# Graph layer with residual normalisation: 64 edges of each later part with a low source node fetched from a table in SBUF by one-hot products

## The chip, the cores and the metric

The kernel runs on one core of one Trainium2 chip. The metric is device time in microseconds of that core, the median of several runs. One profiled execution is shown beside it; all durations below come from that one.

## The reference, cut to what matters

12,500 nodes with 128 features, 412,500 edges sorted by destination (200,000 random pairs in both directions, and a self-loop for each node, which is the last edge of its destination).

```python
theta = x[dst] - x[src]
w = sigmoid(relu(theta @ W1 + b1) @ W2 + b2)          # W2 has one column
agg = segment_sum(w * theta, dst, num_segments=n_nodes)
indeg = segment_sum(ones, dst, num_segments=n_nodes)
x = layernorm(x + agg + indeg * (x @ W4 + b4))
```

All is float32. A self-loop has theta = 0, so it adds 1 to `indeg` and nothing else.

## The kernel before

A table `z` of 12,500 rows is made first, in 13 chunks (`table_chunk`): each row holds `x @ W1` and `x`, 256 numbers, 1 KB, and is written to DRAM. Since theta @ W1 is a difference of two such rows, an edge needs one gathered row of `z` for its source; what it needs of its destination comes from a window of 96 nodes.

Edges are taken in 394 *parts*. A part fills up to 8 tiles of 128 edges. The first 32 parts (`PLAIN`) hold 1024 edges each. A later part covers `CE` = 1050 edges of which at most 1024 remain, because self-loops are squeezed out. Two parts make a *block* (197 blocks), and a block has one window of 96 destination nodes.

The steps of a part, by the name of the helper and its lines:

- `gather(s)` (L281): one indirect DMA for each tile, issued from GpSimd (POOL), brings 128 rows of `z` into a buffer of `zbuf`. There are `NZ` = 10 such buffers, each as large as one part. Parts 0 to 7 gather `x` instead, two parts to a buffer, since the table is not ready; `both` computes their products.
- `window(b)` (L507 to L536): transposes the 96 nodes' features, multiplies by W1 and W4, and spreads the destination rows with small one-hots `pick` into `y3`. Its products use the PSUM tile `pw`, of which there is one.
- `one_hot(s, half)` (L554, L556): for each half part, TensorE broadcasts the destination offsets into the PSUM tile `pd` (also one), and VectorE compares them into the one-hot `oh`.
- `spread_y(s)` (L565): `oh` times `y3` puts each edge's destination row into the PSUM tile `ph` (two of them).
- `one_hot_w(s)` (L573): a one-hot `ow` from edges to the 96 nodes.
- `weights(s)` (L607 to L614): VectorE subtracts the gathered row (L607), multiplies relu of it by W2 (L608) and sums (L611); ScalarE takes the sigmoid (L612) and scales the 8 tiles by it into `wx` (L614).
- `add_up(s)` (L633): TensorE adds `ow` times `wx` into the block's PSUM tile `pa`; `total(b)` normalises and stores the block.

Gathers run `AHEAD` = 4 parts ahead in the text of the loop; on the chip POOL goes on as long as a buffer of `zbuf` is free, which is when L607 and L614 of the part that had it are done.

The later parts need their self-loops squeezed out before they can be gathered. `place(i, ...)` does that for a *set* of up to 128 parts at once, one part to a partition: it marks edges, and then shifts the kept ones to the left by 1, 2, 4, ... places in 6 passes over chunks of 210 columns (L422, L424, L426: three VectorE instructions for a chunk). It is a generator; the loop over parts takes four steps of it a part for the first set and one step a part for the others, so that its work lies between that of the parts. At its end ScalarE and TensorE turn the result into `src_i` (the gathers' indices), `rel` and `off`. There are three sets; the first is needed by the gathers of part 32.

The order on each engine is made by a scheduler from this program; SP's queue alone keeps the order of the text. At the end a flag, made of checks on the indices (`bad`), decides whether a general path (`any_dst`) computes everything once more.

Of the kernel before, what the change touches and what calls it, by code (L numbers as in the profile page):

```python
# [20 lines left out]
K = 8  # L21
# [7 lines left out]
TG = 7  # L29
NZ = 10  # L30
AHEAD = 4
# [3 lines left out]
PLAIN = 2 * FIRST  # L35
CE = 1050
BIG = 1 << 16
# [5 lines left out]
def gnn_resnorm(  # L43
# [11 lines left out]
    out: bass.AP,  # L55
):


# [64 lines left out]
    def load(i):  # L123

        s0, n, full = sets[i]
        es = ep.tile([P, CE], I32, name="es")
        ed = ep.tile([P, CE + 1], I32, name="ed")
        e0 = E1 + (s0 - PLAIN) * CE
        if full < n:
            nc.vector.memset(es[:n, :], 0)  # L130
            nc.vector.memset(ed[:n, :], N)
        for t, edges, m in ((es, src, CE), (ed, dst, CE + 1)):
            nc.sync.dma_start(t[:full, :m], bass.AP(
                tensor=edges.tensor, offset=edges.offset + e0, ap=[[CE, full], [1, m]]))
            if full < n:
                nc.sync.dma_start(
                    t[full:n, :TAIL], edges[E - TAIL:E].rearrange("(s e) -> s e", s=1))
        bb = ep.tile([P, 1], I32, name="bb")
        with nc.allow_non_contiguous_dma(reason="each block's first dst"):
            nc.sync.dma_start(bb[:n], bass.AP(  # L140
                tensor=dst.tensor, offset=dst.offset + e0, ap=[[SUB * CE, n // SUB], [0, SUB], [1, 1]]))
        return es, ed, bb
# [56 lines left out]
    def constants():  # L199
# [57 lines left out]
        nc.vector.tensor_scalar(at, at, -4.0, None, op0=OP.add)  # L257
        return place_c, one_c, m12, m2, yu_buf, behind, ones_b, b4_3


    wx_buf = [const.tile([P, K, AW], F32, name=f"wx{i}") for i in range(3)]
    for t in wx_buf:
        nc.vector.memset(t[:, :, D + 1:], 1.0)

    zbuf = [const.tile([P, K, 2 * D], F32, name=f"zbuf{i}") for i in range(NZ)]
    NX = NH // 2

    def tiles(s):
        return K if s < NF else KT
# [24 lines left out]

    bad = const.tile([P, 12 + 10 * len(sets)], F32, name="bad")
    nc.vector.memset(bad, 0.0)
# [68 lines left out]
    def place(i, ps, es, ed, bb):  # L365

        s0, n, full = sets[i]
        es, ed, bb = es[:n], ed[:n], bb[:n]  # L370
        v = nc.vector
        c = ep.tile([P, 6], F32, name="col")[:n]
# [6 lines left out]
        v.tensor_sub(c[:, 3:4], nxt, d0)  # L379
        b = bad[:n, 12 + 10 * i:22 + 10 * i]  # L380
        v.tensor_scalar(b[:, 0:1], c[:, 3:4], -float(SW - 1), None, op0=OP.add)
        v.tensor_scalar(b[:full, 1:2], c[:full, 3:4], -1.0, float(CE - BE), op0=OP.mult, op1=OP.add)
        v.tensor_scalar(b[:, 2:3], c[:, 2:3], -1.0, -float(NOT), op0=OP.mult, op1=OP.add)
# [7 lines left out]
        for j in range(3):  # L391
            at = slice(j * C, (j + 1) * C)
            step = ps.tile([P, G, P], F32, name="pw").rearrange("p g d -> p (g d)")[:n, :C]
            v.tensor_sub(step, ed[:, j * C + 1:(j + 1) * C + 1], ed[:, at])
            q = ep.tile([P, C], F32, name="eq")[:n]
            v.tensor_sub(q, es[:, at], ed[:, at])
            yield
            v.tensor_mul(q, q, step)
            v.scalar_tensor_tensor(t[:, at], step, 0.0, t[:, at], op0=OP.is_equal, op1=OP.mult)
            nc.scalar.activation(step, step, AF.Square, accum_out=b[:, 4 + j:5 + j])  # L400
            nc.scalar.activation(q, q, AF.Square, accum_out=b[:, 7 + j:8 + j])
            yield
# [4 lines left out]
        v.memset(b[:, 5:7], 0.0)  # L407
        w = ep.tile([P, CE], I32, name="ew0")[:n]
        v.tensor_add(w, t, es)
        yield  # L410
        def half(w, h):
            return w.bitcast(U16).rearrange("p (e h) -> p e h", h=2)[:, :, h]

        C = CE // 5
        for r in range(SW.bit_length()):
            u = ep.tile([P, CE], I32, name=f"ew{1 - r % 2}")[:n]
            m = 1 << r
            for c0 in range(0, CE, C):
                c2 = min(c0 + C + m, CE)
                c1 = c2 - m  # L420
                bit = bits[:n, :c2 - c0]
                v.tensor_scalar(bit, w[:, c0:c2], BIG.bit_length() - 1 + r, 1,  # L422
                                op0=OP.logical_shift_right, op1=OP.bitwise_and)
                v.scalar_tensor_tensor(u[:, c0:c2], bit, 0.0, w[:, c0:c2],  # L424
                                       op0=OP.is_equal, op1=OP.mult)
                v.copy_predicated(u[:, c0:c1], bit[:, m:m + c1 - c0], w[:, c0 + m:c1 + m])  # L426
                yield
            w = u
        off = pp.tile([P, BE], BF16, name="off")
        nc.scalar.activation(off[:n], half(w, 1)[:, :BE], AF.Identity, bias=c[:, 1:2])  # L430
        t = ep.tile([P, CE], F32, name="et")[:n]
        nc.scalar.activation(t[:, :BE], half(w, 1)[:, :BE], AF.Identity, bias=c[:, 2:3])
        yield
        src_i = pp.tile([P, K, P], I32, name="src_i")
        rel = pp.tile([P, K, P], F32, name="rel")
        f = ep.tile([P, CE], F32, name="es")[:n]
        nc.scalar.activation(f[:, :BE], half(w, 0)[:, :BE], AF.Copy)
        yield
# [10 lines left out]
    with tc.manual_schedule(engines={SP}), tc.tile_pool(name="work", bufs=2) as wp, tc.tile_pool(  # L449
# [57 lines left out]
        def window(b):  # L507
# [14 lines left out]
            for h in range(ns):  # L522
# [12 lines left out]
                                           op0=OP.mult, op1=OP.add)  # L535
            d.update(y3=y3, u=yu[:, 1, :])  # L536

# [30 lines left out]
        def one_hot_w(s):  # L568

            n = tiles(s)  # L570
            (_, rel, _), i = set_of(s)
            ow = wp.tile([P, K, WB], F32, name="ow", bufs=4)
            nc.vector.tensor_tensor(  # L573
# [20 lines left out]
        def weights(s):  # L594
# [4 lines left out]
            wx = wx_buf[s % 3]  # L599
            h = wp.tile([P, K, D], F32, name="h")  # L600
            if s < NH:
# [14 lines left out]
            return summed, scaled  # L616

        def add_up(s):
            n = tiles(s)
# [3 lines left out]
            if h == 0:  # L623
                bd["pa"] = ps_l.tile([P, AW], F32, name="pa")
                if carry[0] is not None:
# [4 lines left out]
                                     start=True, stop=False)  # L630
            end = h == SUB - 1 or s == NS - 1
            for k in range(n):
                nc.tensor.matmul(bd["pa"][:WB], d["ow"][:, k, :], wx_buf[s % 3][:, k, :],  # L633
# [45 lines left out]
        def fetch(b):  # L679
            if b < NK:  # L680
                load_block(b)

        xts, done = [], []

# [13 lines left out]
        with after(done[1]):  # L698
            place_first_dst(0, ps_l, dst_f)
            place_c, one_c, m12, m2, yu_buf, behind, ones_b, b4_3 = constants()  # L700
        fetch(0)
# [10 lines left out]
        for i, (s0, _, _) in enumerate(sets):  # L712
            turns[PLAIN // 4 if i == 0 else s0 - P + AHEAD] = i
        steps = iter(())
# [8 lines left out]
        for s in range(NS + 2):  # L723
            if s in turns:
                edges[s + 3] = turns[s], load(turns[s])
            if s in edges:
                i, loaded = edges.pop(s)
                steps = place(i, ps_l, *loaded)
            for _ in range(4 if s < PLAIN else 1):
                next(steps, None)  # L730
            if s + AHEAD < NS:
# [13 lines left out]
            if s < NS:  # L745
                weighted = weights(s)
            if s + 2 < NS and tiles(s + 2) > G:
                one_hot(s + 2, 1)
            if s > 1:
                with after(weighted if s == NS else [rooted[0]] if s > NS else []):  # L750
                    add_up(s - 2)


# [198 lines left out]
```

## Time and profile before

| | us |
|---|---|
| Median of 3 runs (lowest, highest) | 3978.15 (3977.43, 3979.46) |
| The profiled execution | 3977.41 |
| Its span | 3975.6 |
| Busy: PE, DVE | 2208.2, 2853.7 |
| Busy: ACT, POOL | 1634.7, 2988.3 |
| First and last gather start | 4.1, 3949.6 |

PE is TensorE, PEld its weight load, DVE VectorE, ACT ScalarE, POOL GpSimd, SP SyncE. A line of the page's groups has the source line, the engine, the operation, what it writes and reads, the shapes and the count; after the first bar the busy time in all and the mean in ns of one; after the second the idle time of that engine just before these instructions, and what ended most of it. The line PEclk gives the granted TensorE clock in tenths for 40 equal slices of the span. The granted clock over the whole execution was 0.689 of full.

### The profile page before, as it was taken

To read this page: it belongs to the slowest core of one execution; us is meant where nothing else is said; L and a number is where in the kernel's file an instruction comes from. 1 tells how busy PE (TensorE), PEld (TensorE's weight loads), DVE (VectorE), ACT (ScalarE), POOL (GpSimd) and SP (SyncE) were. 2 spreads that over 40 slices of the span, in tenths; PEclk is the share of its full clock that TensorE was granted. 3 is DMA by queue.
4 is the path that set the end of the run, shared out by engine and by line. 5 is a ranking of instruction groups with operands and counts; after the bars stand their busy time and mean duration, and the time that the engine had idled before them with its cause. 6 is when DMAs were issued, how large, how long until landed. Compare 5 with 4: busy or idle time off the path is not lost.

```text
span 3975.6 us, 46634 instructions
## 1 busy us (share of the span) xinstructions
PE 2208.2 (56%) x12940; PEld 1759.9 (44%) x12941; DVE 2853.7 (72%) x4838; ACT 1634.7 (41%) x5158; POOL 2988.3 (75%) x3159
## 2 busy tenths in 40 slices
PE   6757665655555555556555555555555555555554
PEld 5645444444444444444444444444444444444443
DVE  4798887766666666777776666667666666666675
ACT  3535544443344343444443434433443333344343
POOL 7777777777777777777777777777777777777775
PEclk7867776666666666666666666666666666666666
DMA  7434333333333333433333333333333333333333
GB/s 259 118 110 118 114 111 110 111 111 109 111 110 110 111 110 111 119 107 110 111 109 112 110 111 110 111 109 111 111 110 111 110 110 111 111 110 110 111 111 87
DMA packets 201597, 454.17 MB, mean 114 GB/s; under 512 B 58355, under 2 KB 97755, under 8 KB 199791
## 3 DMA queue, kind: packets, MB, share of 16 engines
q0 software_dynamic: 150176, 408.88, 35.8%
q1 hardware_dynamic: 49181, 35.83, 2.9%
q10 hardware_dynamic: 1970, 6.40, 0.5%
q8 instruction: 104, 1.70, 0.2%
q14 instruction: 166, 1.36, 0.1%
HBM read 428.40 MB, written 22.48 MB: 113 GB/s over the span
## 4 chain that ended last, share of the span: by engine, by line
DVE 42%; DMA 25%; ACT 22%; PE 6%; issue 4%; DVEq 0%; POOL 0%; SPq 0%; ACTq 0%; POOLq 0%
DMA zbuf<-z,src_i 24%; ACT wx L614 18%; DVE ph L607 11%; DVE lg L611 10%; DVE h L608 10%; DVE oh L556 5%; ACT wx L612 3%; PE pa L633 2%; DVE pw L530 2%; DVE y L534 2%; DVE ow L573 1%; DVE o L675 1%; DMA z<-zbuf 1%; PE ph L592 1%; DVEq L607 0%
## 5 line engine op out<-in xcount | busy, mean ns | idle before, releaser
L281 POOL DMA_INDIRECT zbuf<-z,src_i x2894 | 2743.7, 948 | 881.6 <-issue 481.0
L607 DVE TENSOR_TENSOR ph<-ph,zbuf 128x1024 f32<-128x1024 f32 (+1 forms) x386 | 474.8, 1230 | 983.3 <-DMA zbuf<-z,src_i 983.0
L633 PE MATMUL pa<-wx,ow 128*96 128x130 f32 x6300 | 1036.7, 332 | 16.8 <-DVE ow L573 12.8
L633 PEld LDWEIGHTS pa<-wx,ow 128*96 128x96 f32 x6300 | 1009.4, 212 | 48.7 <-DVE ow L573 14.1
L614 ACT ACTIVATE wx<-zbuf,wx 128x128 f32<-128x128 f32 x3150 | 964.0, 388 | 12.2
L565 PEld LDWEIGHTS <-oh 128*128 128x128 bf16 x3086 | 264.2, 112 | 1464.7 <-issue 1393.0
L565 PE MATMUL ph<-y,oh 128*128 128x128 bf16 x3086 | 338.7, 252 | 883.0 <-DVE y L534 777.2
L556 DVE TENSOR_SCALAR oh<-pd,place_c,one_c 128x512 bf16<-128x512 f32 (+1 forms) x788 | 612.9, 778 | 34.6 <-PE ph L590 25.4
L554 PE MATMUL pd<-off,ident_b 128*128 128x512 bf16 (+1 forms) x723 | 351.1, 486 | 510.0 <-DVE oh L556 505.0
L611 DVE TENSOR_REDUCE lg<-h 128x8 f32<-128x1024 f32 x394 | 475.9, 1208 | 2.0 <-ACT wx L612 1.9
L608 DVE SCALAR_TENSOR_TENSOR h<-ph,w_r 128x1024 f32<-128x1024 f32 (+1 forms) x386 | 468.8, 1214 | 0.0
L573 DVE TENSOR_TENSOR ow<-fix,rel 128x768 f32<-128x768 f32 x394 | 371.0, 942 | 0.0
L642 ACT ACTIVATE a<-pa 96x130 f32<-96x130 f32 x197 | 54.3, 276 | 733.1 <-PE pa L633 733.1
L612 ACT ACTIVATE wx<-lg,b_c 128x8 f32<-128x8 f32 x394 | 120.9, 307 | 494.4 <-DVE lg L611 464.5
L532 ACT ACTIVATE ym<-pw 128x256 bf16<-128x256 f32 x197 | 75.4, 383 | 485.4 <-DVE pw L530 483.7
L527 PE MATMUL pw<-yu,pick 99*128 99x128 f32 x788 | 201.6, 379 | 113.0 <-ACT wx L612 49.2
L515 PE MATMUL pw<-wts,xwT 128*96 128x256 f32 x394 | 202.3, 611 | 55.6 <-ACT xwT L513 55.1
L281 POOL DMA_INDIRECT zbuf<-z,src x192 | 182.8, 952 | 58.5 <-issue 33.2
L527 PEld LDWEIGHTS pw<-yu,pick 99*128 99x128 f32 x788 | 145.7, 241 | 157.7 <-issue 58.0
L513 ACT ACTIVATE xwT<-pw 128x96 f32<-128x96 f32 x197 | 49.0, 249 | 278.7 <-PE pw L511 278.4
L629 PEld LDWEIGHTS pa<-a,sh 96*96 96x96 f32 x392 | 96.7, 268 | 125.2 <-DVE sh L627 67.6
L629 PE MATMUL pa<-a,sh 96*96 96x130 f32 x392 | 128.5, 430 | 37.7 <-DVE sh L627 33.9
(161 smaller groups left out, 1912.7 us busy)
## 6 DMA issues: line engine op xcount, KB each, us to landing
zbuf<-z,src_i POOLq DMA_INDIRECT x2894
z<-zbuf SPq DMA_DIRECT2D x12, 1024.0 KB
xw<-in_x_dram SPq DMA_DIRECT2D x197, 48.0 KB
out_dram<-o SPq DMA_DIRECT2D x197, 48.0 KB
zbuf<-in_x_dram ACTq DMA_DIRECT2D x12, 512.0 KB
zbuf<-z,src POOLq DMA_INDIRECT x192
ed<-in_dst_dram SPq DMA_DIRECT2D x2, 525.5 KB
es<-in_src_dram SPq DMA_DIRECT2D x2, 525.0 KB
```

What stands on the lines that cost most here:

```text
L281: nc.gpsimd.indirect_dma_start(out=rows_of(s)[:, k, :], out_offset=None, in_=z if s >= NH else x, in_offset=IndirectOffsetOnAxis(ap=src_i[ ...
L527: nc.tensor.matmul(py[:, h, :], pick[:YB], yb[:YB], start=True, stop=True)
L554: nc.tensor.matmul(pd[:, :n1 - n0, :], ident_b[:m, i:i + 1].to_broadcast([m, P]), off[:, n0 * P:n1 * P], start=True, stop=True)
L556: nc.vector.tensor_scalar(parts[s]["oh"][:, n0:n1, :], pd[:, :n1 - n0, :], place_c, one_c, op0=OP.is_equal, op1=OP.max)
L565: nc.tensor.matmul(d["ph"][:, k, :], d["oh"][:, k, :], blocks[b]["y3"][:, h, :], start=True, stop=True)
L573: nc.vector.tensor_tensor(ow[:, :n, :], iota_f.to_broadcast([P, n, WB]), rel[:, :n, i:i + 1].to_broadcast([P, n, WB]), op=OP.is_equal)
L607: nc.vector.tensor_sub(ph, ph, zs[:, :n, :D])
L608: nc.vector.scalar_tensor_tensor(h[:, :n, :], ph, 0.0, w2_f.to_broadcast([P, n, D]), op0=OP.max, op1=OP.mult)
L611: summed = nc.vector.tensor_reduce(lg[:, :n], h[:, :n, :], AX.X, OP.add)
L612: nc.scalar.activation(wx[:, :n, D], lg[:, :n], AF.Sigmoid, bias=b2_c)
L614: scaled = nc.scalar.activation(wx[:, k, :D], xs[:, k, :], AF.Copy, scale=wx[:, k, D:D + 1])
L633: nc.tensor.matmul(bd["pa"][:WB], d["ow"][:, k, :], wx_buf[s % 3][:, k, :], start=h == 0 and k == 0 and carry[0] is None, stop=end and k = ...
```

## The change

A later part now covers 1116 edges. At least 28 self-loops are squeezed out of it as before, and 64 more edges (`HS`) whose source is below 1152 (`HOT` = 128 x 9) are taken out of the gather. So 1024 are gathered still, in 341 later parts rather than 362: 373 parts, 187 blocks, and again three sets.

`place` finds the 64: it forms a key of each edge with a low source, and takes the eight largest keys of a part (`max`) and strikes them out (`match_replace`), eight times. It then counts, for every kept edge, by how many places it has to move (a scan), and the shifting has 7 passes over chunks of 224 columns rather than 6 over 210. The first set is begun after part 4 rather than part 8, with five steps a part.

The first 1152 rows of `z` are loaded into SBUF once (`hot_t`, 9 rows on each partition). For each block from the 17th on (171 blocks) there are four new helpers: `hot_one_hot` broadcasts the block's 128 hot edges' source and destination into PSUM (`pd`) and compares them into nine one-hots `of` and one `to`; `hot_rows` fetches the rows by nine f32 products, and adds the destination's row, in the PSUM tile `pw`; `hot_weights` forms the weight and the scaled row `wxh`, and a one-hot `owh`; `add_up` adds one more product into `pa`.

To make room, `NZ` goes from 10 to 9, the one-hot `ow` has three buffers instead of four, and `h` is written over `ph` in PSUM instead of into SBUF.

```diff
-NZ = 10
+NZ = 9
...
-CE = 1050
+HS = 64
+HT = 9
+HOT = P * HT
+CE = 1116
+PM = 31
...
+    hot_t = const.tile([P, HT, 2 * D], F32, name="hot_t")
...
-        w = ep.tile([P, CE], I32, name="ew0")[:n]
-        v.tensor_add(w, t, es)
+        v.tensor_add(t, t, es)
         yield
...
+        v.tensor_tensor(
+            key.rearrange("p (a m) -> p a m", m=PM), t.rearrange("p (a m) -> p a m", m=PM),
+            apart[:n].rearrange("p (o m) -> p o m", o=1).to_broadcast([n, CE // PM, PM]), op=OP.add)
+        yield
+        v.scalar_tensor_tensor(key, es, float(HOT), key, op0=OP.is_lt, op1=OP.mult)
+        yield
+        top = ep.tile([P, HS], F32, name="top")[:n]
+        for j in range(0, HS, 8):
+            v.max(top[:, j:j + 8], key)
+            yield
+            v.match_replace(key, top[:, j:j + 8], key, -1.0)
+            yield
...
+        for j in range(6):
...
+            v.scalar_tensor_tensor(keep, key[:, at], 0.0, kept, op0=OP.is_ge, op1=OP.mult)
+            v.scalar_tensor_tensor(w[:, at], t[:, at], float((2 * NOT - 1) * BIG), keep,
+                                   op0=OP.min, op1=OP.mult)
+            v.tensor_scalar(out_, keep, -1.0, 1.0, op0=OP.mult, op1=OP.add)
+            v.tensor_tensor_scan(count, out_, most[:n].to_broadcast([n, C]),
+                                 c[:, 4:5] if j else 0.0, op0=OP.add, op1=OP.min)
...
-        for r in range(SW.bit_length()):
+        for r in range((SW + HS).bit_length()):
...
-            ow = wp.tile([P, K, WB], F32, name="ow", bufs=4)
+            ow = wp.tile([P, K, WB], F32, name="ow", bufs=3)
...
-            h = wp.tile([P, K, D], F32, name="h")
+            h = d["ph"]
...
+        def hot_one_hot(b):
+            (hr, _), j = hot_set(b)
+            d = blocks[b]
+            n = hr.shape[0]
+            pd = ps_l.tile([P, G, P], F32, name="pd")
+            col = pair[:n, j:j + 1].to_broadcast([n, P])
+            nc.tensor.matmul(pd[:, :2, :], col, hr[:, :2, :], start=True, stop=False)
+            nc.tensor.matmul(pd[:, 0, :], col, hr[:, 2, :], start=False, stop=True)
+            d["of"] = wp.tile([P, HT, P], F32, name="of", bufs=1)
+            nc.vector.tensor_tensor(
+                d["of"], pd[:, 0:1, :].to_broadcast([P, HT, P]),
+                nid.rearrange("p (t o) -> p t o", o=1).to_broadcast([P, HT, P]), op=OP.is_equal)
+            d["to"] = wp.tile([P, P], F32, name="to", bufs=1)
+            nc.vector.tensor_scalar(d["to"], pd[:, 1, :], place_w, one_w, op0=OP.is_equal, op1=OP.max)
+
+        def hot_rows(b):
+            d = blocks[b]
+            d["px"] = ps_l.tile([P, G, P], F32, name="pw")[:, :2, :]
+            for t in range(HT):
+                nc.tensor.matmul(d["px"], d["of"][:, t, :], hot_t[:, t, :], start=t == 0, stop=False)
+            nc.tensor.matmul(d["px"][:, 0, :], d["to"][:YB], d["yb"][:YB], start=False, stop=True)
+
+        def hot_weights(b):
+            (_, hrel), j = hot_set(b)
+            d = blocks[b]
+            wx = d["wxh"] = wxh_buf[b % len(wxh_buf)]
+            h = wp.tile([P, D], F32, name="hh", bufs=1)
+            lg = wp.tile([P, 1], F32, name="lgh")
+            nc.vector.scalar_tensor_tensor(
+                h, d["px"][:, 0, :], 0.0, w2_r, op0=OP.max, op1=OP.mult, accum_out=lg)
+            nc.scalar.activation(wx[:, D:D + 1], lg, AF.Sigmoid, bias=b2_c)
+            nc.scalar.activation(wx[:, :D], d["px"][:, 1, :], AF.Copy, scale=wx[:, D:D + 1])
+            d["owh"] = wp.tile([P, WB], F32, name="owh", bufs=3)
+            nc.vector.tensor_scalar(d["owh"], fix[:, :WB], hrel[:, j:j + 1], None, op0=OP.is_equal)
...
             end = h == SUB - 1 or s == NS - 1
+            if end and b in hot_blocks:
+                nc.tensor.matmul(bd["pa"][:WB], bd["owh"], bd["wxh"], start=False, stop=False)
...
-            turns[PLAIN // 4 if i == 0 else s0 - P + AHEAD] = i
+            turns[PLAIN // 8 if i == 0 else s0 - P + AHEAD] = i
...
-            for _ in range(4 if s < PLAIN else 1):
-                next(steps, None)
+            if s == NH:
+                nc.sync.dma_start(
+                    hot_t, z[:HOT, :].rearrange("(p t) d -> p t d", t=HT))
+                nc.scalar.activation(hot_t[:, :, :D], hot_t[:, :, :D], AF.Copy, scale=-1.0)
+            if s % 2 == 0 or s < PLAIN - 3:
+                for _ in range(5 if s < PLAIN else 1):
+                    next(steps, None)
...
+            if s % 2 and (s + 1) // SUB in hot_blocks:
+                hot_weights((s + 1) // SUB)
             if s + 2 < NS and tiles(s + 2) > G:
                 one_hot(s + 2, 1)
+            if s % 2 == 0 and s // SUB + 1 in hot_blocks:
+                hot_one_hot(s // SUB + 1)
...
+            if s % 2 == 0 and s // SUB + 1 in hot_blocks:
+                hot_rows(s // SUB + 1)
+            if s % 2 and s > PLAIN - 3:
+                next(steps, None)
```

## The prediction

> **What bounds the kernel now.** I read the page's busy table and slices first, then the groups, then the timeline of one quiet block (two parts) late in the run, then the timeline of the first 350 us.
>
> ```profile
> PE 2208.2 (56%) x12940; PEld 1759.9 (44%) x12941; DVE 2853.7 (72%) x4838; ACT 1634.7 (41%) x5158; POOL 2988.3 (75%) x3159
> PEclk7867776666666666666666666666666666666666
> ```
> ```profile
> L281 POOL DMA_INDIRECT zbuf<-z,src_i x2894 | 2743.7, 948 | 881.6 <-issue 481.0
> L607 DVE TENSOR_TENSOR ph<-ph,zbuf 128x1024 f32<-128x1024 f32 (+1 forms) x386 | 474.8, 1230 | 983.3 <-DMA zbuf<-z,src_i 983.0
> ```
> No engine looks full: POOL shows 75%. But its 25% is 0.30 us in front of every gather, and the timeline (start, length, engine, line, and in brackets the idle time before) shows a metronome:
>
> ```profile
> 3001.20 0.95 POOL L281 DMA_INDIRECT zbuf<-z,src_i  x1 [0.30 <-ACT wx L614]
> 3002.45 0.95 POOL L281 DMA_INDIRECT zbuf<-z,src_i  x1 [0.30 <-issue]
> 3003.70 0.95 POOL L281 DMA_INDIRECT zbuf<-z,src_i  x1 [0.30 <-issue]
> ```
> ```profile
> 3004.10 1.23 DVE L607 TENSOR_TENSOR ph<-ph,zbuf 128x1024 f32<-128x1024 f32 x1 [2.85 <-DMA zbuf<-z,src_i]
> 3014.09 1.23 DVE L607 TENSOR_TENSOR ph<-ph,zbuf 128x1024 f32<-128x1024 f32 x1 [3.24 <-DMA zbuf<-z,src_i]
> 3010.19 3.67 PE L633 MATMUL pa<-wx,ow 128*96 128x130 f32 x16
> 3014.32 1.94 PE L633 MATMUL pa<-wx,ow 128*96 128x130 f32 x16
> ```
> A gather starts every 1.25 us; 3150 of them run from 4.1 to 3949.6 us, 1.2527 us each. Eight make a part, so a part takes 10.0 us. VectorE waits for the gathers at L607 in nearly every part, 983 us in all: POOL's issue sets the pace, and VectorE has 6.1 us to spare in a 20 us block. That spare is what the change spends.
>
> **What it removes.** A later part covers 1116 edges, not 1050 (1024 gathered, 64 hot, at least 28 self-loops left out): 379,732 edges past the first 32 parts make 340 full parts and a tail of 292 (3 tiles), before 361 and 682 (6 tiles). Gathers: 372 x 8 + 3 = 2979 against 3150, 171 fewer, x 1.2527 = **-214.2 us** if POOL stays the bound. Of the work per part, 21 parts fewer fall away too, at about 7 us of VectorE each; off the path.
>
> **What each block gains (171 blocks).** VectorE: the one-hot `of` (128x1152 out of PSUM, nearest row L573, 768 columns 0.94: scaled by columns beside a fixed 0.14, 1.34), `to` 0.4, the row sum `hh` 0.5, `owh` 0.3; neighbours in the trace start about 0.08 before the last one's end, so 2.2 us. `h` stays in PSUM: L608 (reads PSUM) 1.215 against L611 (SBUF) 1.208, so 0 to 0.1. 13.9 us of VectorE (the window below) becomes 16.2 of 20.
> ScalarE: 0.31 + 0.39, hidden (41% busy).
> TensorE: nine f32 products with 256 columns, two passes each. L515 (same width) gives 0.22 us a pass at full clock (0.67 for two with 0.2 of latency), 0.43 at half: 18 passes are 4.1 or 7.9 us, with `to`, `owh` and the index broadcasts 4.8 or 9. The two L633 rows above show the two speeds in one block: 0.121 and 0.229 us an instruction. [...] The rows are windows: length, busy us of PE, PEld, DVE, ACT and POOL, granted clock, DMA share, GB/s.
>
> ```profile
> 160.00:180.00 20.00, 17.78 (x167) 15.27 (x165) 19.08 (x30) 14.30 (x50) 15.12 (x17) 1.00 0.38 108
> 3000.00:3020.00 20.00, 10.81 (x62) 8.94 (x62) 13.91 (x23) 7.43 (x26) 15.13 (x17) 0.66 0.38 110
> ```
>
> **The new waits.** In the changed order VectorE does L607's successor, `of`, `to`, then `ow`, h, the reduce, `o`, two `pick` (4.3 us), then `hh`, which waits for all the hot rows; behind `hh` stand both one-hots of the next part, and the next L607. TensorE often puts one part's L633 products (1.94) before or amid the hot rows. With a part landing at 0: `of` ends at 2.4, rows are ready at 7.4 to 9.1, VectorE arrives at 6.7: a wait of 0.7 to 2.4. `hh` also holds the single `pw` bank, behind which the next window's transposes queue, and the `yh` that VectorE wants comes some 3.3 us after them: 1.0 to 1.5 more (before, L530 waits 1.4 there when it runs late). Block period of this loop: 18.2 to 19.9 us, against POOL's 20.04. POOL still leads, by little. Cost: 0 in the free blocks; without the cover, the excess over 20.04 times 171.
>
> **Placement (three sets).** One compaction instruction costs 0.30 us net (L422 to L426: 0.38 less overlap). Before: 90 of them, 12 of 0.43, the rest, 35 us a set. After: 105 x 0.31 = 33; eight maxima and eight replacements over 1116 columns, nearest row L409 (1.25), 1.2 and 1.35: 20; 48 instructions to mark, count and pack, 0.25: 12; twelve of 0.46, three of 1.25, small ones: 14. Sum 79, **44 more a set**.
>
> *Set 0* is where there is no cover:
> ```profile
> 297.48 0.36 DVE L426 COPY_PREDICATED ew<-fix,ew 128x178 int32<-128x178 int32 x1
> 303.59 0.58 ACT L445 ACTIVATE src_i<-pw 128x512 int32<-128x512 f32 x1
> 315.62 1.22 DVE L607 TENSOR_TENSOR ph<-ph,zbuf 128x1024 f32<-128x1024 f32 x1
> 325.47 0.94 POOL L281 DMA_INDIRECT zbuf<-z,src_i  x1 [0.30 <-issue]
> ```
> By the first window row above VectorE is full from 160 us on (19.1 of 20), and works on part 8 while POOL issues part 16. Placement is done at 304, gathers of part 32 need it at 324: 20 us to spare. Buffers: POOL may be 10 parts ahead, now 9 (`NZ`). Adding the new work in the changed order, part 22 starts behind a clump of 47 placement rows at about 349 us (before, part 24 after such a clump at 315.6), its buffer is free 6 us or more later, and part 31's gathers, due at 314 in the same slots, start at about 355: **+41 us** that nothing returns, since POOL is the bound afterwards. Ends: +15 (placement fills VectorE's idle time before 160 us) and +60. The load of the hot table (1.2 MB on SP's queue, ScalarE waits for it once) lies in the same stretch and in those ends.
>
> *Sets 1 and 2* add 2 steps, 1.9 us, to 67 blocks: 20 to 21.5 us. VectorE falls back up to 1.5 us a block; buffers take some 35 us for set 1 and about as much for set 2. I take **+20** for both; ends 0 and +90.
>
> [...]
> ```profile
> 482.24 1.24 DVE L409 TENSOR_TENSOR ew<-et,es 128x1050 int32<-128x1050 f32 x1
> 482.54 1.76 POOL L281 DMA_INDIRECT zbuf<-z,src_i  x1 [0.30 <-ACT wx L614]
> ```
> The addition of two SBUF tensors lengthens the gather beside it by 0.81 of its 1.24 us. [...]
>
> **Tail.** The last part has 3 tiles, not 6: -2 us of VectorE, ScalarE and TensorE work.
>
> **Sum.** Profiled execution 3977.4 (span 3975.6; the median of the runs is 3978.15, 0.7 above): 3977.4 - 214.2 + 41 + 20 + 12 - 2 = **3834**. 0.2%, 8 us, is about what a measurement of this kernel can tell from no change.
>
> **Rivals.**
> *Early stall covered* (0.14): placement hides in VectorE's waits before 160 us, the sets cost nothing: 3977.4 - 214.2 + 12 - 2, 3773 to 3800. For it: VectorE is busy only 38 of the 80 us from 80 to 160 (windows of 20 us). Against: only 16 placement rows stand before part 8.
> *VectorE leads during placement* (0.22): 22.5 us in 67 blocks, 2.5 x 67 = 167, less 35 of buffers, for 20: +112, about 3946; 3870 to 3986.
> *The loop through the hot rows leads throughout, slower than before* (0.20): at the half clock `hh` is ready at 11 to 14, not 7.4 to 9.1, and the block takes 22 to 24 us. The gain less the fixed costs is 214 - 41 - 12 + 2 = 163, over 171 blocks 0.95: from a mean period of 21.0 us the change loses; at 22 it gives 4150. For it: the clock of 0.68 in steady rows, and only 0.1 to 1.8 us between my walk and 20.04. Against: a VectorE that runs late leaves TensorE no idle window, and the row at 160 us had clock 1.00.
> *It doesn't gather less* (under 0.01): a flag that sends the program down the general path. The inputs hold 75 to 131 eligible edges in every full part, and 64 are needed.
>
> **Numbers.** Likeliest (0.44): 3834, own range 3805 to 3870. Faster: 0.14 + 0.44 + 0.18 of the second rival = 0.76; same 0.04; slower 0.20. Range 3775 to 4000, which leaves out the worse part of the loop rival and a little below.
>
> **What would show it.** Right: 2979 gathers, 1.25 us apart outside the first 400 us; a gap of some 40 us on POOL between 190 and 370; VectorE still waiting for gathers at the subtract in the last third, its busy share above 80%; TensorE's clock above 0.8. Wrong: the gathers of the last third more than 10.1 us a part, with VectorE's largest wait at `hh` on the hot-row products; or no early gap.

## The result and the profile after

The changed kernel takes 3816.02 us (median of 4 runs, 3814.91 to 3817.94) against 3978.81 (3977.43 to 3980.45): a ratio of 0.9591, 95% interval 0.9575 to 0.9608. The forecast was 3834. The profiled execution has a span of 3816.2 us, where the one before had 3975.6. Six of the runs below (e1 to e4, e10, e11) were made on a chip where the kernel before itself takes 5258 to 5262 us; they are told, but no figure of theirs is set beside the others. Beside e5 to e9 and e12 the kernel before takes 3976.1 to 3977.9 us, so a difference of 2 or 3 us between one of them and the change tells nothing.

The busy table, the slices of TensorE's clock and the groups of the page after:

```profile
PE 2819.9 (74%) x16390; PEld 2317.8 (61%) x16390; DVE 3215.7 (84%) x5794; ACT 1657.3 (43%) x5239; POOL 2829.8 (74%) x2988
PEclk7866877877788888887877787788888778787787
...
L321 POOL DMA_INDIRECT zbuf<-z,src_i x2723 | 2584.2, 949 | 829.7 <-issue 441.8
...
L751 PE MATMUL pw<-hot_t,of 128*128 128x256 f32 x3078 | 807.3, 420 | 64.5 <-DVE of L740 57.7
...
L713 DVE TENSOR_TENSOR ph<-ph,zbuf 128x1024 f32<-128x1024 f32 x365 | 448.3, 1228 | 59.3 <-DMA zbuf<-z,src_i 57.2
```

The gather is still 0.949 us and the subtract (L713, before L607) still 1.23. What has changed is the idle time in front of the subtract: 57 us, where it was 983: nearly all of VectorE's waiting for gathers is gone. The hot rows (L751) are 807.3 / 171 = 4.7 us of TensorE a block. The same block as before, in the table of windows:

```profile
3000.00:3020.00 20.00, 15.49 (x90) 12.86 (x90) 15.90 (x29) 8.54 (x29) 15.12 (x17) 0.79 0.37 109
```

TensorE rose from 10.8 to 15.5 us of 20, VectorE from 13.9 to 15.9; POOL stands at 15.1 as before. POOL's timeline shows where it stopped (start, length, and in brackets the idle time before):

```profile
181.82 0.94 POOL L321 DMA_INDIRECT zbuf<-z,src  x1 [11.27 <-ACT wx L720]
...
209.90 0.94 POOL L321 DMA_INDIRECT zbuf<-z,src  x1 [3.40 <-ACT wx L720]
...
259.19 0.94 POOL L321 DMA_INDIRECT zbuf<-z,src  x1 [9.22 <-ACT wx L720]
...
315.96 0.94 POOL L321 DMA_INDIRECT zbuf<-z,src  x1 [6.96 <-ACT wx L720]
...
328.25 0.94 POOL L321 DMA_INDIRECT zbuf<-z,src  x1 [2.59 <-ACT wx L720]
...
362.59 0.94 POOL L321 DMA_INDIRECT zbuf<-z,src  x1 [14.39 <-ACT wx L720]
```

Each of these gathers waited for the last reader of its buffer, ScalarE's scaling L720 of the part nine before it. Less the usual 0.30 in each, the six gaps are 11.0 + 3.1 + 8.9 + 6.7 + 2.3 + 14.1 = 46.1 us. After 363 us POOL never stops again.

The account from span to span: 171 gathers fewer, at 1.25 us, are -213.75; the six gaps +46.1; gathers lengthened by other engines +3.2 (all excess of gather distances over 1.25 us is 58.5 after and 9.2 before; 49.3 less 46.1); and from the last gather to the end it takes 31.0 us instead of 26.0, +5.0. Together -159.4, which is 3975.6 to 3816.2.

A quantity that the page does not print explains most of what follows: the *backlog* of a part, from the start of its last gather to the start of its subtract, both read from the timeline (us).

| part | 8 | 12 | 24 | 36 | 60 | 110 | 170 | 230 | 300 |
|---|---|---|---|---|---|---|---|---|---|
| before | 68.1 | 60.5 | 61.4 | 25.3 | 3.0 | 2.9 | 2.9 | 3.0 | 2.9 |
| after | 66.0 | 91.0 | 90.1 | 37.0 | 49.0 | 62.4 | 6.5 | 36.4 | 3.1 |
| e5, set 0 early | 111.2 | 143.9 | 18.2 | 3.3 | 22.6 | 36.4 | 3.0 | 33.2 | 3.0 |
| e6, 7 buffers | 63.3 | 88.5 | 68.8 | 18.4 | 27.4 | 40.2 | 2.8 | 33.1 | 3.1 |
| e12, 48 plain parts | 68.1 | 73.7 | 69.0 | 58.7 | 26.9 | 45.9 | 14.7 | 36.5 | 7.6 |

Before, VectorE has caught up at part 50 and then takes each part 2.9 us after its last gather. After, it catches up only at about part 289; it is behind through both later sets (its backlog grows where a set is placed, about parts 40 to 110 and 180 to 236, and shrinks elsewhere), and the ring of buffers hides that.

VectorE's largest waits after, over the whole run (total, times, longest):

```profile
DVE ow L679 <- PE pa L784: 151.9, 113, 3.3
DVE pw L636 <- ACT yh L635: 118.9, 140, 2.1
DVE hh L760 <- PE pw L752: 87.2, 86, 3.4
DVE ph L713 <- DMA zbuf<-z,src_i: 57.2, 42, 5.1
```

The wait for gathers has become three kinds of short wait inside the loop, each found 86 to 140 times in the 187 blocks.

### The profile page after: what moved, and what is told of

It reads as the page before. It is cut to its first block, busy times and chain, and to the rows that moved or that the text cites. A ratio compares the mean times of both kernels' runs of the same rounds, so it can differ in the third digit from the quotient of the medians.

```text
span 3816.2 us, 54171 instructions
## 1 busy us (share of the span) xinstructions
PE 2819.9 (74%) x16390; PEld 2317.8 (61%) x16390; DVE 3215.7 (84%) x5794; ACT 1657.3 (43%) x5239; POOL 2829.8 (74%) x2988
## 4 chain that ended last, share of the span: by engine, by line
PE 45%; DVE 25%; ACT 11%; DMA 8%; issue 8%; POOL 2%; DVEq 0%; SPq 0%; ACTq 0%; POOLq 0%
PE pa L784 15%; PE pw L751 15%; DMA zbuf<-z,src_i 7%; ACT wx L720 4%; DVE oh L662 4%; DVE lg L717 3%; PE pw L633 3%; DVE ph L714 3%; DVE ph L713 3%; PE pw L621 3%; PE pd L660 2%; DVE of L740 2%; DVE ow L679 2%; POOL zbuf L321 2%; PE pa L778 2%
## 5 line engine op out<-in xcount | busy, mean ns | idle before, releaser
L321 POOL DMA_INDIRECT zbuf<-z,src_i x2723 | 2584.2, 949 | 829.7 <-issue 441.8
L784 PE MATMUL pa<-wx,ow 128*96 128x130 f32 x5958 | 976.4, 322 | 47.9 <-DVE ow L679 25.3
L784 PEld LDWEIGHTS pa<-wx,ow 128*96 128x96 f32 x5958 | 908.6, 202 | 85.9 <-ACT wx L720 28.8
L720 ACT ACTIVATE wx<-zbuf,wx 128x128 f32<-128x128 f32 x2979 | 917.1, 388 | 10.2
L751 PE MATMUL pw<-hot_t,of 128*128 128x256 f32 x3078 | 807.3, 420 | 64.5 <-DVE of L740 57.7
L751 PEld LDWEIGHTS pw<-hot_t,of 128*128 128x128 f32 x3078 | 639.9, 215 | 174.0 <-DVE of L740 73.5
L662 DVE TENSOR_SCALAR oh<-pd,place_c,one_c 128x512 bf16<-128x512 f32 (+2 forms) x745 | 579.8, 778 | 74.1 <-PE pd L660 46.1
L718 ACT ACTIVATE wx<-lg,b_c 128x8 f32<-128x8 f32 (+1 forms) x373 | 114.4, 307 | 1104.9 <-DVE lg L717 1034.0
L713 DVE TENSOR_TENSOR ph<-ph,zbuf 128x1024 f32<-128x1024 f32 x365 | 448.3, 1228 | 59.3 <-DMA zbuf<-z,src_i 57.2
L679 DVE TENSOR_TENSOR ow<-fix,rel 128x768 f32<-128x768 f32 (+1 forms) x373 | 352.2, 945 | 151.9 <-PE pa L784 151.9
L717 DVE TENSOR_REDUCE lg<-ph 128x8 f32<-128x1024 f32 (+1 forms) x373 | 451.6, 1211 | 2.0 <-ACT wx L718 2.0
L714 DVE SCALAR_TENSOR_TENSOR ph<-ph,w_r 128x1024 f32<-128x1024 f32 x365 | 445.7, 1221 | 0.0
L740 DVE TENSOR_TENSOR of<-pd,nid 128x1152 f32<-128x1152 f32 x171 | 229.9, 1345 | 1.2 <-PE pd L738 1.2
L633 PEld LDWEIGHTS pw<-yu,pick 99*128 99x128 f32 x746 | 121.8, 232 | 68.1 <-ACT yu L624 61.4
```

The costliest lines, as they stand in the source:

```text
L321: nc.gpsimd.indirect_dma_start(out=rows_of(s)[:, k, :], out_offset=None, in_=z if s >= NH else x, in_offset=IndirectOffsetOnAxis(ap=src_i[ ...
L633: nc.tensor.matmul(py[:, h, :], pick[:YB], yb[:YB], start=True, stop=True)
L662: nc.vector.tensor_scalar(parts[s]["oh"][:, n0:n1, :], pd[:, :n1 - n0, :], place_c, one_c, op0=OP.is_equal, op1=OP.max)
L679: nc.vector.tensor_tensor(ow[:, :n, :], iota_f.to_broadcast([P, n, WB]), rel[:, :n, i:i + 1].to_broadcast([P, n, WB]), op=OP.is_equal)
L713: nc.vector.tensor_sub(ph, ph, zs[:, :n, :D])
L714: nc.vector.scalar_tensor_tensor(h[:, :n, :], ph, 0.0, w2_f.to_broadcast([P, n, D]), op0=OP.max, op1=OP.mult)
```

## The experiments

**e5: place set 0 early.** (e2 is the same kernel.) VectorE has idle time before 150 us; can it pay for set 0?

```diff
-            turns[PLAIN // 8 if i == 0 else s0 - P + AHEAD] = i
+            if i:
+                turns[s0 - P + AHEAD] = i
...
+        early = load(0)
...
-        steps = iter(())
+        steps = place(0, ps_l, *early)
...
-                for _ in range(5 if s < PLAIN else 1):
+                for _ in range(9 if s < NH else 5 if s < PLAIN else 1):
```

> Set 0's edges are loaded ahead of the rest of the table, and its placement starts with part 0 instead of part 7, nine steps a part up to part 8, then five; nothing else changes. Its instructions on VectorE are then done before part 9 instead of part 23. Theory (the 46 us of early stall are placement work in a stretch where VectorE is full, and before 150 us VectorE has some 40 to 60 us of idle time): the stall falls to 0 to 15 us, 3770 to 3786. Rival A (the stall is caused by the hot table's load and scaling, or by the changed later blocks): 3816. Rival B (the work falls into the chain of the first eight parts, which TensorE leads, and only delays them): VectorE's backlog at part 8 grows from 66 us to 100 or more and the stall stays at 40 or grows, 3810 to 3840.

> The same kernel as in e2 (set 0's edges loaded ahead of the table, its placement begun with part 0, nine steps a part, then five), run again, because on the chip of e1 to e4 the kernel before itself took 5262 us instead of 3978: TensorE waited there for its own instructions (weight loads that stood 0.7 to 2 us apart with nothing to wait for), so that those four runs say nothing of POOL's pace. Where the kernel before takes 3978 us: theory (the 46 us of early stall are placement work in a stretch where VectorE is full, and before 150 us it has 40 to 60 us of idle time), the stall falls to 0 to 15 us, 3770 to 3786. Rival A (the stall comes from the hot table's load and scaling or from the changed later blocks): 3816. Rival B (the work falls into the chain of the first eight parts, which TensorE leads): 3810 to 3840. If the kernel before again takes far over 3978, none of the three is tested.

e2: 5789.38 us, where the kernel before took 5262.32; no test. e5: 3856.36 us, ratio 0.9694 (0.9678 to 0.9711), 40 us more than the change. Rival B had the mechanism, though its range ended at 3840: part 8's subtract starts at 206.6 instead of 159.2 us, its backlog is 111 instead of 66, and POOL loses 87.0 us in gaps instead of 46.1, more than half of it in one:

```profile
209.45 0.94 POOL L321 DMA_INDIRECT zbuf<-z,src  x1 [0.30 <-issue]
258.81 0.94 POOL L321 DMA_INDIRECT zbuf<-z,src  x1 [48.42 <-ACT wx L720]
```

VectorE's idle time there was slack between the steps of a chain that TensorE leads (`both`, parts 0 to 7). In VectorE's fixed order the placement stood ahead of steps that TensorE waited for, in clumps: 50 placement instructions between the products with W2 of parts 1 and 2, 37 more before part 3's, and 52 between the subtract of part 8 (206.6 us) and part 7's product with W2 (253.3 us), which stands behind it in VectorE's order. In this last stretch TensorE's transposes of the finished placement (L549) also stand ahead of part 7's own (L691), which use the same tile `pw`:

```profile
236.05 1.12 PE L549 MATMUL pw<-ident,es 128*128 128x128 f32 x4
...
244.51 1.11 PE L691 MATMUL pw<-ident,zbuf 128*128 128x128 f32 x4 [0.69 <-ACT rel L551]
```

The 48 us gap waits for this part. So idle time of an engine inside another engine's chain is not free for long clumps of work. Once the clumps are over, the backlog falls to 3 us by part 36, and then it stays under 40 through set 1.

**e6: 7 buffers in the ring.** (e1 is the same kernel.)

```diff
-        return zbuf[(s - NH + NX) % NZ]
+        return zbuf[(s - NH + NX) % 7]
```

> Only the ring of gather buffers changes: parts from 8 on use 7 of the 9 buffers. Theory (POOL's only stalls are VectorE's backlog of set 0's placement meeting the end of the ring; later the backlog stays inside it): a part's gathers wait once the subtract comes more than about 74 us after the last gather with 9 buffers, so about 54 with 7. The early stall of 46 us becomes 66, and the backlog that enters set 1 is 20 us smaller, so set 1, which brought it to 74 with 9 buffers, brings it to 54 and costs 0 to 5 us: 3836, 3830 to 3845. Rival A (the early stall comes from the load and scaling of the hot table or from the SP queue, not from the buffers): 3816, no change. Rival B (the block loop itself needs the buffers, since its parts are freed late): each block loses some tenths of a us all through, 3850 or more, with gaps on POOL spread over the run.

> The same kernel as in e1 (parts from 8 on use 7 of the 9 gather buffers), run again where the kernel before takes its 3978 us. Theory (POOL's only stalls are VectorE's backlog of the start and of set 0's placement meeting the end of the ring; a part's gathers wait once the subtract comes more than about 74 us after that part's last gather with 9 buffers, so about 54 with 7): the early stall of 46 us becomes 66; the backlog that enters set 1 is 20 us smaller, so set 1, whose backlog peaked at 74 with 9 buffers, peaks at 54 and costs 0 to 5 us: 3836, 3830 to 3845. Rival A (the early stall comes from the hot table's load, not from the buffers): 3816. Rival B (the loop needs the buffers all through): 3850 or more, with gaps on POOL spread over the run.

e1: 5765.64 us on the chip of e2; no test. e6: 3830.89 us, ratio 0.9631 (0.9615 to 0.9647), 14.9 us more than the change, where 20 were forecast. The gaps before 363 us sum to 62.3, 16.2 more; nothing stops POOL later. So the buffers are what the early stall is measured against. Set 1 costs nothing even with 7: POOL's longer stall at the start leaves a backlog that is 20 us smaller, 15.7 instead of 36.1 at part 40, and set 1 adds 26 to that; the peak is 42.2, at part 111. The two expectations above took the peak with 9 buffers for 74; it is 64.3.

**e7: set 0 without its maxima and replacements.**

```diff
+        if i == 0:
+            v.memset(top, 0.0)
-        for j in range(0, HS, 8):
+        for j in range(0, HS if i else 0, 8):
```

> Set 0 alone is placed without the eight maxima and eight replacements (which hot edges it has is left out: its parts get wrong ones, and the flag for the general path is kept at zero); sets 1 and 2 and all block work are as in the changed kernel. It takes 16 instructions of 1.31 us, 21 us, of VectorE away between 170 and 250 us. Theory (the early stall of 46 us is a shortage of VectorE time before part 31, so each us saved there is a us of POOL): stall 25, 3795 (3788 to 3803). Rival A (the stall is set by the hot table's load and scaling, or by TensorE's slow clock in that stretch): 3812 to 3818. Rival B (the maxima hold more than themselves, as TensorE's chain waits behind them): 3770 to 3787.

The flag for the general path is held at zero by one more line, since the parts of set 0 get wrong hot edges. 3798.15 us, ratio 0.9551 (0.9535 to 0.9567): 17.9 us less than the change for 21 us of VectorE work left out. POOL's gaps before 330 us sum to 27.9, 18.2 fewer. In this stretch VectorE's time is POOL's time, nearly one for one.

**e8: `ow` with both inputs in SBUF.**

```diff
-                ow[:, :n, :], iota_f.to_broadcast([P, n, WB]),
+                ow[:, :n, :],
+                iota_row[:, :WB].rearrange("p (o m) -> p o m", o=1).to_broadcast([P, n, WB]),
```

> The one-hot for the scatter, ow, compares the same numbers, but reads them from iota_row in SBUF and not from their copy in PSUM: 373 instructions of 0.945 us, before with one SBUF input, now with two. VectorE's time should not change. [...] Rival A (only the few long operations of the placement collide, since the three sets together lengthened gathers by under 10 us): 3816 to 3835. Rival B (ow itself gets slower): its mean rises above 1.0 us and VectorE leads.

The estimate was 3926 to 4056 us, worked out from two additions of SBUF tensors that lengthened a gather: L409 before, by 0.81 us, and L451 after, by 1.10. 3927.55 us, ratio 0.9874 (0.9857 to 0.9890): 111.5 us more than the change, at the low end of that range. `ow` itself keeps its 0.945 us, the gather's mean goes from 949 to 995 ns:

```profile
L321 POOL DMA_INDIRECT zbuf<-z,src_i x2723 | 2708.1, 995 | 829.4 <-issue 427.6
...
L679 DVE TENSOR_TENSOR ow<-iota_row,rel 128x768 f32<-128x768 f32 (+1 forms) x373 | 352.8, 947 | 106.5 <-PE pa L785 106.1
```

POOL's busy time is up by 134.7 us (2829.8 to 2964.5). Part of that comes back: POOL is stopped for 30.6 us at the start instead of 46.1, and from the last gather to the end it takes 20.4 us instead of 31.0. Together +108.6, where the spans differ by 108.4. Two pairs of the timeline show when a gather is hit:

```profile
2521.21 1.89 POOL L321 DMA_INDIRECT zbuf<-z,src_i  x1 [0.30 <-ACT wx L719]
...
2521.36 0.92 DVE L679 TENSOR_TENSOR ow<-iota_row,rel 128x768 f32<-128x768 f32 x1
...
3010.17 0.95 POOL L321 DMA_INDIRECT zbuf<-z,src_i  x1 [0.30 <-ACT wx L721]
...
3010.79 0.94 DVE L679 TENSOR_TENSOR ow<-iota_row,rel 128x768 f32<-128x768 f32 x1
```

An `ow` that starts 0.15 us into a gather adds 0.94 to it, its own whole length; one that starts 0.62 us in leaves it at 0.95. Sorted by that distance, the 340 `ow` after 420 us show: of 102 that start in a gather's first 0.36 us, 41 lengthen it, mostly by 0.8 to 1.1 us; of 99 that start 0.36 to 0.65 us in, 5 do. A start at about 0.8, 1.0 or 1.2 us adds 0.37, 0.55 or 0.6 to the next gather on average: of the first two, what is left of the `ow` when the gather starts, less 0.13 us; the third is 0.17 short of that. So in e8 the collision lies mostly in the first 0.36 us of a gather. Why the other 61 early starts did no harm stays open.

**e9: the loop without POOL's bound.** (e3 is the same kernel.)

```diff
-        for k in range(tiles(s)):
+        for k in range(tiles(s) if s < PLAIN + 8 else min(tiles(s), 6)):
```

> The changed kernel, but from part 40 on only 6 of a part's 8 tiles are gathered; the rows of the other two are an earlier part's. A block's gathers then take 15.0 us instead of 20.04, and the block loop runs at its own pace. Theory (that pace is 18.2 to 18.6 us, read from the rate at which VectorE's backlog shrinks, 0.93 and 0.7 us a part, and about 20.8 in the blocks that place): parts 40 to 371 take 99 x 18.4 + 67 x 20.8 = 3215 us, the end comes near 3750 us (3700 to 3780), VectorE hardly waits for gathers. Rival A (the pace is nearer to 20, POOL and the loop being just balanced): 3800 or more. Rival B (TensorE at full clock makes the loop much shorter than 18): below 3650.

> The same kernel as in e3 (from part 40 on only 6 of a part's 8 tiles are gathered; the rows of the other two are an earlier part's), run again where the kernel before takes its 3978 us. A block's gathers take 15.0 us, so the block loop runs at its own pace. Theory (18.2 to 18.6 us in blocks that place nothing, read from the rate at which VectorE's backlog shrinks; 20.8 where a set is placed): 99 x 18.4 + 67 x 20.8 = 3215 us for parts 40 to 371, the end near 3750 us (3700 to 3780), VectorE hardly waits for gathers. Rival A (the pace is nearer to 20, POOL and the loop just balanced): 3800 or more. Rival B (TensorE at full clock makes the loop much shorter): below 3650.

e3: 4816.68 us on the chip of e2; no test. e9, one run: 3767.17 us, inside the 3700 to 3780 of the theory. A quarter of the gathers of each part from 40 on is left out, and it gains only 49 us. No wait of VectorE for gathers stands among its largest, and POOL waits for buffers all through (960.4 us of waits for L720, where the changed kernel has 249.6):

```profile
POOL zbuf L321 <- ACT wx L720: 960.4, 673, 14.3
```

From the starts of L713, a block takes 20.6 and 20.7 us where a set is placed (parts 56 to 110, 184 to 236), and 18.1, 18.85 and 19.1 elsewhere (parts 112 to 170, 240 to 300, 300 to 340). In the changed kernel itself the same stretches take 20.6, 20.7, 18.1, 19.0, and 20.1 for parts 300 to 340, where it has caught up. So the loop is 1 to 2 us a block faster than POOL without placement, and 0.6 to 0.7 slower with it.

**e4 and e11: the same cut in the kernel before** (6 and 5 tiles of 8).

```diff
+        for k in range(tiles(s) if s < PLAIN + 8 else min(tiles(s), 5)):
```

> The kernel before, with the same cut: from part 40 on, 6 of a part's 8 tiles are gathered. Theory (before, POOL alone set the pace, the loop's own work was 13.9 us of VectorE a block): 353 full parts x 2 x 1.2527 = 884 us fewer, 3093 us, if the loop keeps up with 15.0 us a block; 3093 to 3250 if the loop needs up to 15.9. Rival (the loop before had a pace of its own near 18 us through its waits on TensorE and ScalarE, so that the hot rows cost little of it): 3600.

> The kernel before, but from part 40 on only 5 of a part's 8 tiles are gathered (the rows of the other three are an earlier part's): a block's gathers take 12.5 us instead of 20.04, and the block loop without hot rows runs at its own pace. Theory (14.4 us a block, read from the rate at which VectorE's backlog shrank before, 2.8 us a part between parts 24 and 40; two sets of 35 us come on top): 353 x 7.2 + 70 = 2610 us for parts 40 to 393, the end near 3060 us (3000 to 3150). So the hot rows would have lengthened the loop by about 4 us a block, though they give VectorE only 2.2 us of work. Rival (the loop before was already near 16.5 us by its waits, the hot rows add little more than VectorE's 2.2): 353 x 8.25 + 70, the end near 3430 us.

4324.45 and 3798.65 us, where the uncut kernel before took 5262.32 and 5258.41. Neither tests the pace of the old loop. What is left is the rate at which its backlog shrank between parts 24 and 40, 2.8 us a part.

**e12: 48 plain parts.** (e10 is the same kernel.) If the stall is a shortage of VectorE time before a date, move the date.

```diff
-PLAIN = 2 * FIRST
+PLAIN = 3 * FIRST
...
+            place_first_src(2 * FIRST, ps_l, src_h)
+            place_first_dst(2 * FIRST, ps_l, dst_h)
...
-                for _ in range(5 if s < PLAIN else 1):
+                for _ in range(3 if s < PLAIN else 1):
```

> 48 instead of 32 plain parts at the start (of 1024 edges, placed the simple way), so that set 0 is due 16 parts (160 us) later, and its placement takes 3 steps a part instead of 5. Price: 373 full parts and one of 6 tiles, 2990 gathers instead of 2979, 13.8 us of POOL. Theory (the early stall of 46 us is VectorE's shortage of time before set 0 is due; a plain part takes VectorE 7.2 us where it is free, 79 us of placement over 33 parts add 2.4, together 9.6, under POOL's 10.02, so that the backlog of some 64 us at part 8 does not grow to the 74 at which POOL stalls): stall 0 to 10, 3816 - 46 + 14 + 0 to 10 = 3784 to 3794. Rival A (the stall is a matter of clumps in VectorE's order, not of the mean): half of it stays, 3800 to 3810. Rival B (it has another cause in the first 400 us): 3826 to 3832.

> The same kernel as in e10 (48 plain parts at the start, set 0's placement 3 steps a part), run again because the kernel before itself took 5258 us in e10 and e11. Price: 11 more gathers, 13.8 us of POOL. Theory (the early stall of 46 us is VectorE's shortage of time before set 0 is due; 7.2 us a plain part and 2.4 of placement stay under POOL's 10.02, so that the backlog of 64 us at part 8 does not grow to the 74 at which POOL stalls): stall 0 to 10, 3816 - 46 + 14 + 0 to 10 = 3784 to 3794, and the backlog that enters set 1 is under 40 us. Rival A (the stall is a matter of clumps in VectorE's order, not of the mean): half of it stays, 3800 to 3810. Rival B (it has another cause in the first 400 us): 3826 to 3832.

e10: 5769.83 us, before 5258.41; no test. e12: 3782.88 us (3781.20 to 3785.04), ratio 0.9513 (0.9497 to 0.9528), 33.1 us less than the change although it issues 11 gathers more. It is the fastest kernel of this study. The longest wait of POOL for a buffer is 1.3 us, where it was 14.4:

```profile
POOL zbuf L323 <- ACT wx L722: 199.3, 651, 1.3
```

The backlog stands at 68 to 76 us from part 8 to part 24; the 76.1 of part 20 is what stops POOL for 1.0 us beyond its usual 0.30. It is about 20 us when set 1 begins, at part 52; under 40 was expected. From span to span the stall gives 45.1 us and the end 5.3 (25.7 us after the last gather); the 11 gathers take 13.75 and lengthened gathers 3.0 more: together -33.6.

## Why the prediction was right

*POOL stays the bound, -214.2.* Right. 2979 gathers, 1.25 us apart after 363 us; with that distance the term is -213.75. e9 shows how narrow it was: with POOL out of the way the loop needs 18.1 to 19.1 us in blocks that place nothing, against POOL's 20.04. The walk said 18.2 to 19.9.

*What a block gains.* VectorE 13.9 to 15.9 or 16.1 us (160.6 in the 200 us from 3000), forecast 16.2. Hot rows on TensorE 4.7 us, near the 4.1 of the full clock and far from 7.9. The walk, with the rows ready at 7.4 to 9.1, counts on the full clock; that TensorE would run them so was the author's estimate. Measured: the granted clock rose from 0.689 to 0.802, and from 0.66 to 0.79 in the 20 us from 3000, with TensorE busy for 15.5 us of them instead of 10.8. The waits were smaller than walked: `hh` 0.5 us a block on average (forecast 0.7 to 2.4), `yh` 0.6 (1.0 to 1.5). One was missed: `ow` waits 0.8 us a block for L784, the scatter products that last read its buffer. That TensorE works those off behind the hot rows, and that `ow` has three buffers instead of four, both bear on it; which does was not tried.

*The early stall, +41.* 46.1, and part 31's gathers start at 362.6 us (forecast 355), part 22's subtract at 355.0 (349). A set takes VectorE 77 to 83 us, less overlaps, where 79 were forecast. The mechanism is the one named: e7 takes 21 us of VectorE out and gets 17.9 back, e6 takes two buffers away and pays 14.9, e12 moves the date and gets the whole stall back. The shape was wrong: not one gap but six, from 170 us on, since the first placement steps already stand before parts 8 and 10 and bring the backlog to 90 by part 10. The sum fits all the same: VectorE does not wait for a gather between 160 and 363 us, so its own work sets when part 22's buffer comes free, and the earlier gaps are shares of that one delay. The rival of the covered stall counted on VectorE's idle time before 160 us; e5 shows that this time cannot be had by starting earlier in such clumps.

*Sets 1 and 2, +20.* They cost 0. The step "VectorE falls back up to 1.5 us a block" is the term that failed: it falls back 0.6 to 0.8 (20.6 and 20.7 against 20.04 in the stretches of e9, and 28 us over the 36 blocks from part 40, with a backlog of 36.1, to part 111, with 64.3), and the ring takes it up. Some 12 us were left: in e12 the first stall comes at a backlog of 76.1. The second rival (22.5 us a block while placing) had the right place and the wrong size; the third needed 21.0 as a mean.

*Gathers lengthened by VectorE, +12.* The account leaves 3.2 for it. No run shows the 12; it was the author's estimate. What the runs show in its place: in the changed kernel the gathers that start while L451 runs (two SBUF inputs, 1.31 us) take 2.09, 2.04 and 1.38 us instead of 0.95, one in each set, and in e8 each `ow` costs POOL 0.36 us on average. But of the short operations with two SBUF inputs that the change adds (L502 and L510, 36 of 0.34 us), 9 start in a gather's first 0.36 us, and one of these gathers takes over 1.0 us; and three of the long ones in set 0 (L451, L455, L459, from 167.1 to 171.1 us) fell beside a POOL that then stopped for 11.27 us, for L720.

*The tail, -2.* It is +5.0. The last subtract starts 3.6 us after the last gather in both kernels. But in the changed one VectorE does it, with a wait for its rows, before the product with W2 (L714) of the part before, so that the work of two parts stands behind the last landing:

```profile
3785.19 0.95 POOL L321 DMA_INDIRECT zbuf<-z,src_i  x1 [0.30 <-issue]
...
3788.83 0.57 DVE L713 TENSOR_TENSOR ph<-ph,zbuf 128x384 f32<-128x384 f32 x1 [2.78 <-DMA zbuf<-z,src_i]
3789.30 1.22 DVE L714 SCALAR_TENSOR_TENSOR ph<-ph,w_r 128x1024 f32<-128x1024 f32 x1
```

In e8, whose order has that product first, the end takes 20.4 us.

The profiled execution took 3817.9 us, 16.1 less than the sum: 20 for the sets and 8.8 for the lengthened gathers were too much, 7 for the tail, 5.1 for the early stall and 0.5 for the gathers too little, which leaves 16.2. So the total is nearer than its terms: errors of 28.8 us one way and 12.6 the other.

*The signs.* VectorE's busy share in the last third is 81%, and the wait at the subtract is there (57.2 us, all after 2600 us), but it is no longer the largest: `ow` has 58.6 in the same stretch. Read strictly, that sign was weaker than announced.

## What to carry to other kernels

An engine's spare time is spent first where it has none: cost a change over the whole run, then again over the stretch where the engine that pays is full and behind. Plot the backlog between producer and consumer by item; while it is above its floor, its slope tells the consumer's own pace, and its ceiling is the ring; both can be read without a further run. If a deadline causes the stall, moving the deadline (e12) can be worth more than starting earlier (e5).

## What the runs showed of the hardware

In e8 a gather from GpSimd was held up by a VectorE operation with two SBUF inputs that was running when the gather started (by 0.37, 0.55 and 0.6 us on average where it had started 0.8, 1.0 and 1.2 us into the gather before), or that started within the gather's first 0.36 us (41 of 102, mostly for 0.8 to 1.1 us); of those that started 0.36 to 0.65 us in, 5 of 99 did it. The 373 operations of 0.945 us cost POOL 0.36 us each on average.

On the chip of e1 to e4, e10 and e11, TensorE stood idle in front of products for which the profile shows no engine to wait for: 634 us in 335 such gaps in e1, where the changed kernel has 8 us in 4. In e4, the products of one part:

```profile
3061.16 0.22 PE L565 MATMUL ph<-y,oh 128*128 128x128 bf16 x1
3063.26 0.22 PE L565 MATMUL ph<-y,oh 128*128 128x128 bf16 x1 [1.88 <-issue]
3063.96 0.22 PE L565 MATMUL ph<-y,oh 128*128 128x128 bf16 x1 [0.48 <-issue]
3065.34 0.22 PE L565 MATMUL ph<-y,oh 128*128 128x128 bf16 x1 [1.17 <-issue]
```

Eight of these take 1.0 us elsewhere in the same trace. The change, with 16,390 TensorE instructions instead of 12,940, was not run there itself; its variants that gather all rows took 5766 to 5789 us, 1.10 times the kernel before. What held the instructions back was not settled.
